# Layer 0 of a two-layer graph network: where the preparation and output stages stand among a step's matrix products

## The chip, the cores and the metric

The kernel runs on one core of a Trainium2 chip (trn2). The metric is device time in microseconds (us) of one execution; of several executions the median is taken. Five engines work side by side on a core and meet at semaphores: TensorE (PE in the profile, with its weight loads as PEld), VectorE (DVE), ScalarE (ACT), GpSimd (POOL) and SyncE (SP, which issues DMAs here).

## The reference, cut to what matters

The change lies wholly in layer 0, which is a graph attention layer over 3327 nodes with 256 features and 4 heads of 64 features, applied to a normalized input:

```python
h = maximum(layernorm(x), 0)
support = (h @ weight) per head                    # n x 64 for each of 4 heads
f1, f2 = support . weight_u, support . weight_v    # one number per node and head
e = exp(leaky_relu(f1[None, :] + f2[:, None], 0.2) - row maximum), where adj != 0, else 0
out = (e / sum of e over the row) @ support + bias + h @ proj_w.T + proj_b
x = x + out
```

Layer 1 (two steps of attention cut to its largest weights, with a second, smoothing path over the graph) takes the rest of the time and isn't touched.

The kernel uses that exp(leaky_relu(z)) is max(exp(z), exp(0.2 z)). A factor that belongs to the row alone cancels in the division, so the weight of neighbour j for node i is exp(0.2 f1[j]) times max(exp(0.8 f1[j]), exp(-0.8 f2[i])). The tiles are named `eas` for exp(0.2 f1), `cf` for exp(0.8 f1) and `ef` for exp(-0.8 f2), which is spread over the partitions into `xf0`.

## The kernel before, in words

Layer 0 works on the transposed matrix: partitions are 128 neighbours j (26 tiles, the last of 127 rows), columns are nodes i. The columns come in four blocks (`BLOCKS`) of 6, 8, 8 and 4 tiles, that is 768, 1024, 1024 and 511 columns. The main loop (L961) runs over `order`: 4 blocks times 26 tiles j, 104 steps. The sums over j are held in PSUM for the whole of a block.

A step does this, in the order in which it is written:

- The adjacency tile for three steps ahead is loaded (`load_adj`, SP queue) and the present one is copied to `adj_r` in DRAM (POOL queue).
- `weigh` (L913, DVE instruction at L920) makes the weights of heads 0 and 1. Each is one DVE instruction over all columns of the block. The weights go round in a ring of seven buffers (`weights`, L661 and L662). In the trace these buffers are called `lg` and `w`. A step uses four of them, so the fourth head of a step (h = 3) takes the buffer that head 0 of the step just before held; heads 0 to 2 take buffers of the step before that one.
- DVE then does what has been put between the heads. In block 0 that is `take(i - 1)` (L740; L742, L748, L749), which moves the features of a later tile from PSUM into `sup` and `res`, and in every second step `stats` (L679; L683 and L684) of two tiles. In blocks 1 to 3 it is what `on_dve` holds for the step (L980): parts of the output of the block before.
- `weigh` makes the weights of heads 2 and 3.
- PE does `sum_features(accs, j, 0)` (L922, product at L928), the weighted sum of features of heads 0 and 1. Two heads stand side by side in 64 columns each of the PE array.
- PE does the preparation and output stages. In block 0 `features(i, 7)` (L710; L714, L716, L718) multiplies a later tile by the layer's weights, i = j + 8. In blocks 1 to 3 it is what `on_pe` holds for the step (L988).
- PE does `sum_features(accs, j, 1)`, the same sum for heads 2 and 3.
- In block 0 PE does `turn(i + 1, 6)` (L698, transposes at L703).
- PE does `sum_weights(accs, j)` (L933, product at L938), the sum of the weights of all four heads, four of them side by side in 32 columns each. It is the last reader of the step's weight buffers.

When a block is finished, its sums are copied out (L1006) and each of its tiles of 128 nodes becomes an `Out`, whose stages are spread over steps of the next block by lines 1008 to 1026: `divide` on PE (L765), a step later `output` on DVE, POOL and ACT (L773 to L788, L790 to L792, L797), then `turn` on PE (L813, copied by ACT at L817), `keys` on PE (L823, ACT L442), `take_keys` on DVE (L444) in the step after, `graph` on PE (L849, ACT L853 and L855) and `take_graph` on DVE (L865) in the step after that. In blocks 1 and 2 this makes a cycle of three steps for each tile: `keys` of one tile with `divide` of the next, then a step with nothing on PE, then `graph` with `turn`. In block 3 eight tiles share 26 steps of half the length, so that steps without any such stage are rare.

The order on PE, DVE, ACT and POOL is the order in which the program is written (`in_traced_order`, L385). An engine whose next instruction has to wait holds up everything behind it. Layer 1's order comes from a planner (`Order`) with costs fixed in the source; it does not depend on the order in layer 0.

Of the kernel before, what the change touches and what calls it, by code (L numbers as in the profile page):

```python
# [312 lines left out]
def kernel(  # L313
# [34 lines left out]
    def rows(i):  # L348
        return min(P, N - i * P)
# [56 lines left out]
    def move_rows(queue, dst, src, pn):  # L406

        for p0, p1 in ((0, pn // 16 * 16), (pn // 16 * 16, pn)):
            if p0 < p1:
                queue.dma_start(out=dst[p0:p1], in_=src[p0:p1])  # L410
# [198 lines left out]
    def bank(k, shape, name="pt"):  # L609
        return banks.tile(shape, FP, tag=f"b{k}", name=name)  # L610
# [14 lines left out]
    if True:  # L625
# [33 lines left out]
        HP = H // 2  # L659
# [19 lines left out]
        def stats(g0):  # L679
            g1 = min(g0 + 2, NT)  # L680
            for i in range(g0, g1):
                st = small.tile([P, 6], FP, tag="ln_st", name="st")
                nc.vector.bn_stats(st, res[:, i, :])  # L683
                nc.vector.bn_aggr(mv[:, i, :], st)  # L684
            g, n = nc.gpsimd, slice(g0, g1)
            g.tensor_scalar(rs[:, n], mv[:, n, 1], EPS, None, ALU.add)
            g.tensor_tensor(rs[:, n], rs[:, n], mhalf.to_broadcast([P, g1 - g0]), ALU.pow)
            g.tensor_tensor(nmr[:, n], mv[:, n, 0], rs[:, n], ALU.mult)
            g.tensor_scalar(nmr[:, n], nmr[:, n], -1.0, None, ALU.mult)
# [3 lines left out]
        def normalize(i):  # L693
            normed[i] = hn = turn_of(spare)
            nc.scalar.activation(
                hn, res[:, i, :], AF.Relu, bias=nmr[:, i : i + 1], scale=rs[:, i : i + 1]
            )
# [12 lines left out]
        def features(i, k):  # L710
            hT, pt = turned.pop(i)
            f1, f2, pw = pt[:, D : D + H], pt[:H, D + H : D + H + P], bank(k, [P, 2, D])
            for c in range(DC):
                nc.tensor.matmul(f1, hT[:, c], wuv[:, c, 0], start=(c == 0), stop=(c == DC - 1))  # L714
            for c in range(DC):
                nc.tensor.matmul(f2, wuv[:, c, 1], hT[:, c], start=(c == 0), stop=(c == DC - 1))  # L716
            for c in range(DC):
                nc.tensor.matmul(pw, hT[:, c], wcat[:, c], start=(c == 0), stop=(c == DC - 1))  # L718
            t0, t1 = next(s for s in SPREADS if s[0] <= i < s[1])
            nc.scalar.activation(eas[:, i], f1, AF.Exp, scale=SLOPE)  # L720
            nc.scalar.activation(cf[:, i], f1, AF.Exp, scale=1.0 - SLOPE)
            nc.scalar.activation(ef[:, i - t0], f2, AF.Exp, scale=SLOPE - 1.0)
            if i == t1 - 1:
                spread(t0, t1, ef)
            made[i] = pw
# [14 lines left out]
        def take(i):  # L740
            pw = made.pop(i)
            nc.vector.tensor_tensor(  # L742
                sup[:, i].rearrange("p (h o) -> p h o", h=H),
                pw[:, 0].rearrange("p (h o) -> p h o", h=H),
                eas[:, i].unsqueeze(2).to_broadcast([P, H, O]), ALU.mult,
            )
            t = pa.tile([P, D], FP, tag="xu", name="t")
            nc.vector.tensor_add(t, pw[:, 1], res[:, i])  # L748
            nc.vector.tensor_add(res[:, i], t, badd)  # L749
# [163 lines left out]
        def weigh(j, at, b, cn, *heads):  # L913
            pj = rows(j)
            for h in heads:
                ws[h] = w = turn_of(weights)
                cw = -(-cn // P) * P
                cb = xf0[b][:pj, :, h * P : (h + 1) * P].bitcast(FP)
                a, o = (t[:pj, :cw].rearrange("p (t n) -> p t n", n=P) for t in (at, w))
                nc.vector.scalar_tensor_tensor(o, cb, cf[:pj, j, h : h + 1], a, ALU.max, ALU.mult)  # L920

        def sum_features(accs, j, p):  # L922
            pj = rows(j)
            for m, acc in enumerate(accs[p]):
                mn = min(512, cn - 512 * m)
                for q in range(2):
                    h = 2 * p + q
                    nc.tensor.matmul(  # L928
                        acc[q * O : (q + 1) * O, :mn], sup[:pj, j, h * O : (h + 1) * O],
                        ws[h][:pj, 512 * m : 512 * m + mn], start=(j == 0), stop=(j == NT - 1),  # L930
                    )
# [14 lines left out]
        def load_adj(b, j):  # L946
            c0, pj = BLOCKS[b][0] * P, rows(j)
            cn = min(BLOCKS[b][1] * P, N) - c0
            ats[b, j] = at = turn_of(rows_of_adj)
            if cn % P:  # L950
                nc.gpsimd.memset(at[:, cn : -(-cn // P) * P], 0.0)
            move_rows(nc.sync, at[:, :cn], adj_t[j * P : j * P + pj, c0 : c0 + cn], pj)
# [8 lines left out]
        for step, (b, j) in enumerate(order):  # L961
            c0 = BLOCKS[b][0] * P
            cn = min(BLOCKS[b][1] * P, N) - c0
            if j == 0:
                ws = {}
                half = range((cn + 511) // 512)
                accs = [[bank(len(half) * p + m, [P, 512]) for m in half] for p in range(HP + 1)]
            at = ats.pop((b, j))
            if step + 3 < len(order):
                load_adj(*order[step + 3])  # L970
            move_rows(
                nc.gpsimd, adj_r[j * P : j * P + rows(j), c0 : c0 + cn], at[:, :cn], rows(j)
            )
            i = j + AHEAD
            weigh(j, at, b, cn, 0, 1)
            if b == 0 and AHEAD < i <= NT:
                take(i - 1)
            if b == 0 and i % 2 == 0 and i + 4 < NT:
                stats(i + 4)
            for f in on_dve.pop(step, ()):  # L980
                f()
            weigh(j, at, b, cn, 2, 3)
            if b == 0 and i + 2 < NT:
                normalize(i + 2)
            sum_features(accs, j, 0)
            if b == 0 and i < NT:
                features(i, 7)
            for f in on_pe.pop(step, ()):  # L988
                f()
            sum_features(accs, j, 1)  # L990
            if b == 0 and i + 1 < NT:
                turn(i + 1, 6)
            sum_weights(accs, j)
            if j < NT - 1:
                continue
            if b == 0:
                ug = p0.tile([P, DC, 2, D], FP, tag="by", name="ug")
                for n in range(STEPS):
                    nc.sync.dma_start(
                        out=ug[:, :, n, :],  # L1000
                        in_=u1t[STEPS - 1 - n].rearrange("(c p) j -> p c j", p=P),
                    )
            for p in range(HP + 1):
                for m, acc in enumerate(accs[p]):
                    mn = min(512, cn - 512 * m)
                    nc.scalar.copy(ot[:, p, 512 * m : 512 * m + mn], acc[:, :mn])  # L1006
            outs = [Out(c0 // P + t, ot, t * P) for t in range((cn + P - 1) // P)]
            if b < NB - 1:
                last = b == NB - 2
                for k, r in enumerate(outs):  # L1010
                    a = step + 1 + (1 + 13 * k // 5 if last else 1 + 3 * k)
                    ka, kb, kc = ((3, 4)[k % 2], (5, 6)[k % 2], 7) if last else (6, 7, 6)
                    g = a + (5 if last or k < WIDE - 1 else 4)
                    for when, f in (
                        (a, lambda r=r, ka=ka: r.divide(ka)),
                        (a + (3 if last else 2), lambda r=r, kb=kb: r.turn(kb)),
                        (a + (4 if last else 3), lambda r=r, kb=kb: r.keys(kb)),
                        (g, lambda r=r, kc=kc: r.graph(kc)),
                    ):
                        on_pe.setdefault(when, []).append(f)  # L1020
                    for when, f in (
                        (a + 1, r.output),
                        (a + (5 if last else 4), lambda r=r: (r.take_keys(), r.store_keys())),
                        (g + 1, lambda r=r: (r.store_sum(), r.take_graph(), r.store_graph())),
                    ):
                        on_dve.setdefault(when, []).append(f)
# [784 lines left out]
```

## Time and profile before

| what | value |
|---|---|
| median of 3 runs | 2047.48 us (2043.74 to 2048.77) |
| the profiled execution's own time | 2044.76 us |
| its span, first to last instruction | 2042.7 us |
| mean granted clock of TensorE | 0.989 |
| busy PE / DVE / ACT / POOL over the span | 1964.5 / 1679.8 / 1305.6 / 782.7 us |
| main loop of layer 0, block 0 (26 steps of 768 columns) | 42.3 to 214.0 us |
| block 1 (26 steps of 1024 columns) | 214.0 to 378.0 us |
| block 2 (26 steps of 1024 columns) | 378.0 to 546.1 us |
| block 3 (26 steps of 511 columns) | 546.1 to 655.5 us |

The block limits are the starts of the first L928 product of each block and the end of the last L938. In the timeline a row is an instruction or several of one kind in a row: its start in us from the start of the span, its duration, the engine, the line, the operation, output and inputs, shapes and count, and in square brackets the idle time of the engine before it with what ended it. Each fp32 product appears as two PE instructions, so eight L928 rows are one `sum_features` of a block of two 512-column halves. PE's instructions overlap by some 0.07 us; where this text gives the length of a stage on PE, it is the time from its first start to the first start of the next stage.

### The profile page before, as it was taken

What the parts mean: (1) busy time and instruction counts of PE and PEld (TensorE: products, weight loads), DVE (VectorE), ACT (ScalarE), POOL (GpSimd) and SP (SyncE); (2) the same over time, 40 slices, a digit from 0 to 9 for tenths busy, and PEclk for the clock granted to TensorE, in tenths of its full rate; (3) what the DMA queues carried; (4) which work ended last, traced back from release to release, by engine and by line L of the source; (5) the groups of instructions that cost most, each with busy time, mean ns of one, the idle gap of its engine ahead of it and who ended that gap; (6) DMA issues with size and microseconds to landing.
All of it is one profiled execution on the core that took longest, in us unless ns stands there. A gap on an engine that the chain in (4) does not pass through costs nothing. (4 is left out here: it accounts for less than half of the span.)

```text
span 2042.7 us, 34326 instructions
## 1 busy us (share of the span) xinstructions
PE 1964.5 (96%) x11474; PEld 1384.4 (68%) x11474; DVE 1679.8 (82%) x3997; ACT 1305.6 (64%) x2014; POOL 782.7 (38%) x1842
## 2 busy tenths in 40 slices
PE   7999999999999799999999999995999999999996
PEld 3343333233223688888888888884889999999995
DVE  5777988988788597888889798944899999999994
ACT  2110100010112889999998999839899999999991
POOL 3230222133233443334443435405545455444442
PEclk9999999999999999999999999997999999999998
DMA  5445566565565643433334343566243444444440
GB/s 182 144 157 168 191 220 229 172 204 190 177 189 155 175 110 99 107 90 78 93 94 113 80 103 79 142 199 199 64 119 99 107 109 106 109 108 103 102 113 23
DMA packets 324157, 270.60 MB, mean 132 GB/s; under 512 B 30260, under 2 KB 300563, under 8 KB 323972
## 3 DMA queue, kind: packets, MB, share of 16 engines
q1 hardware_dynamic: 311284, 222.85, 40.4%
q0 software_dynamic: 11520, 44.81, 6.2%
q8 instruction: 92, 1.51, 0.3%
q14 instruction: 93, 0.76, 0.1%
q10 hardware_dynamic: 1168, 0.67, 0.1%
HBM read 177.79 MB, written 88.62 MB: 130 GB/s over the span
## 5 line engine op out<-in xcount | busy, mean ns | idle before, releaser
L1218 ACT ACTIVATE at<-lg,at 128x3327 fp8e4<-128x3327 f32 x208 | 638.9, 3072 | 5.1 <-POOL at L1178 2.5
L1072 PE MATMUL accr<-xf,adjt 128*128 128x258 f32 (+3 forms) x1352 | 375.6, 309 | 34.3 <-DMA adjt<-adj_r 18.2
L920 DVE SCALAR_TENSOR_TENSOR lg<-xf,cf,at 128x1024 f32<-128x1024 f32 (+4 forms) x357 | 368.3, 1078 | 45.3 <-PE pt L938 44.9
L1073 PE MATMUL accr<-xf,adjt 128*128 128x256 f32 (+1 forms) x1352 | 343.5, 285 | 1.9 <-DMA xf<-xf_d 1.9
L928 PE MATMUL pt<-lg,sup 128*64 128x512 f32 (+3 forms) x1250 | 335.3, 574 | 1.1 <-DVE lg L920 1.0
L1357 PE MATMUL acca<-res,at 128*128 128x256 f32 (+2 forms) x1352 | 321.7, 379 | 0.0
L1357 PE MATMUL acca<-xa,at 128*128 128x256 f32 (+2 forms) x1352 | 321.1, 379 | 0.0
L1072 PEld LDWEIGHTS accr<-xf,adjt 128*128 128x128 f32 (+1 forms) x1352 | 259.5, 192 | 46.4 <-DMA adjt<-adj_r 18.1
L1073 PEld LDWEIGHTS accr<-xf,adjt 128*128 128x128 f32 (+1 forms) x1352 | 260.5, 193 | 9.3 <-DMA xf<-xf_d 2.5
L1357 PEld LDWEIGHTS acca<-res,at 128*128 128x128 f32 (+2 forms) x1352 | 245.3, 190 | 31.2 <-issue 3.4
L1357 PEld LDWEIGHTS acca<-xa,at 128*128 128x128 f32 (+2 forms) x1352 | 245.6, 190 | 28.3
L1152 POOL TENSOR_SCALAR sc<-sc 128x1 f32<-128x1 f32 (+1 forms) x156 | 34.7, 249 | 476.8 <-ACT sc L1150 476.5
L1133 PE MATMUL pg<-k_sb,q 128*128 128x512 f32 (+2 forms) x728 | 209.8, 407 | 3.8 <-ACT lg L1142 3.2
L928 PEld LDWEIGHTS pt<-lg,sup 128*64 128x64 f32 (+1 forms) x1250 | 92.1, 136 | 176.3 <-issue 116.4
L1284 DVE MAX8 v<-lg 128x8 f32<-128x416 f32 (+2 forms) x416 | 209.9, 577 | 0.1
L1346 ACT COPY at<-pt 128x512 f32<-128x512 f32 (+2 forms) x247 | 128.2, 531 | 65.2 <-PE acca L1357 35.8
L938 PE MATMUL pt<-lg,eas 128*32 128x512 f32 (+3 forms) x1250 | 166.4, 568 | 0.0
L1133 PEld LDWEIGHTS pg<-k_sb,q 128*128 128x128 f32 (+1 forms) x728 | 124.7, 189 | 32.6 <-ACT lg L1142 12.2
L1142 ACT COPY lg<-pg 128x512 f32<-128x512 f32 (+2 forms) x249 | 126.7, 571 | 17.3 <-PE pg L1133 14.9
L1275 DVE SCALAR_TENSOR_TENSOR lg<-sup,th 128x3327 f32<-128x3327 f32 (+1 forms) x35 | 128.9, 3682 | 10.1 <-ACT th L1268 9.9
L1336 PE MATMUL pt<-ident,sup 128*128 128x128 f32 (+2 forms) x910 | 129.4, 276 | 4.0 <-DVE sup L1323 3.6
L1323 DVE SCALAR_TENSOR_TENSOR sup<-sup,vm 128x3327 f32<-128x3327 f32 (+1 forms) x35 | 128.9, 3682 | 0.1
(197 smaller groups left out, 3196.0 us busy)
## 6 DMA issues: line engine op xcount, KB each, us to landing
adjt<-adj_r SPq DMA_DIRECT2D x300, 256.0 KB, 3.1
at<-in_adj_t_dram SPq DMA_DIRECT2D x50, 512.0 KB, 4.3
adj_r<-at POOLq DMA_DIRECT2D x50, 512.0 KB, 5.4
at<-in_adj_t_dram SPq DMA_DIRECT2D x25, 384.0 KB, 3.2
adj_r<-at POOLq DMA_DIRECT2D x25, 384.0 KB, 3.2
qk_d<-qk SPq DMA_DIRECT2D x50, 128.0 KB, 2.7
q<-qk_d SPq DMA_DIRECT2D x100, 64.0 KB, 2.4
xf_d<-xf SPq DMA_DIRECT2D x50, 128.0 KB, 4.1
```

Of the source, the lines that this page charges most:

```text
L920: nc.vector.scalar_tensor_tensor(o, cb, cf[:pj, j, h : h + 1], a, ALU.max, ALU.mult)
L928: nc.tensor.matmul(acc[q * O : (q + 1) * O, :mn], sup[:pj, j, h * O : (h + 1) * O], ws[h][:pj, 512 * m : 512 * m + mn], start=(j == 0), st ...
L938: nc.tensor.matmul(acc[h * QP : (h + 1) * QP, :mn], eas[:pj, j, h : h + 1].to_broadcast([pj, QP]), ws[h][:pj, 512 * m : 512 * m + mn], sta ...
L1072: nc.tensor.matmul(r.acc[:pn, :dx], w, xc[:, :dx], start=begin, stop=False)
L1073: nc.tensor.matmul(r.acc[:pn, :D], w, xc[:, DX:], start=False, stop=end)
L1133: nc.tensor.matmul(r.pg[p][:pn, :mn], r.q[:, v, :pn], k_sb[:, m0 : m0 + mn], start=(v == 0), stop=(v == 1),)
L1218: nc.scalar.activation(junk[:pn], r.lg[:pn, :N], AF.Exp, bias=r.at[:pn, 4:], accum_out=r.g[:pn], saturate=False,)
L1275: nc.vector.scalar_tensor_tensor(r.lg[:pn, :N], e, r.th[:pn], e, ALU.is_lt, ALU.mult, accum_out=r.below[:pn])
L1284: nc.vector.max(r.v8[:pn, q], r.lg[:pn, q * w : min((q + 1) * w, N)])
L1323: nc.vector.scalar_tensor_tensor(e, e, r.vm[:pn, 1:], e, ALU.is_ge, ALU.mult, accum_out=kept[:pn])
L1336: nc.tensor.transpose(r.pt[g][: rows(c), j, : r.pn], r.e[: r.pn, c * P : c * P + rows(c)], ident[: r.pn, : r.pn],)
L1357: nc.tensor.matmul(r.acc[: r.pn], wt[: rows(c), j, : r.pn], xa[: rows(c), c, :], start=(c == 0), stop=(c == NT - 1),)
```

## The change

The stages on PE that stood between the two feature sums are put behind both of them, ahead of the sum of weights. The sum of features of heads 2 and 3 follows at once on that of heads 0 and 1; in block 0 `turn(i + 1, 6)` then follows at once on `features(i, 7)`.

```diff
             weigh(j, at, b, cn, 2, 3)
             if b == 0 and i + 2 < NT:
                 normalize(i + 2)
-            sum_features(accs, j, 0)
+            for p in range(HP):
+                sum_features(accs, j, p)
             if b == 0 and i < NT:
                 features(i, 7)
             for f in on_pe.pop(step, ()):
                 f()
-            sum_features(accs, j, 1)
             if b == 0 and i + 1 < NT:
                 turn(i + 1, 6)
             sum_weights(accs, j)
```

The order of instructions on DVE, ACT and POOL is the same in both kernels, and PE has the same products in another order. On SP the store of `p_d` and one of the two stores of `xf_d` change places for three tiles. The moved stages carry with them what they issue on other engines: the exponentials of `features` (L720 to L722) and, in five steps, the five DMAs of `spread` (L727); the copies of `turn`, `keys` and `graph` on ACT.

## The prediction

> **What bounds the kernel now.** I read the busy time by windows first, cut at the limits of the blocks, then the waits between 42.3 and 655.5 us, then the timelines of PE and DVE step by step.
>
> ```profile
> core 0: us, PE busy (x) PEld busy (x) DVE busy (x) ACT busy (x) POOL busy (x), PEclk, DMA share, GB/s
> 42.30:180.70 138.40, 138.40 (x826) 54.85 (x826) 97.99 (x156) 20.50 (x86) 35.89 (x49) 1.00 0.45 142
> 546.10:655.50 109.40, 109.25 (x529) 30.66 (x525) 89.59 (x183) 17.20 (x45) 37.52 (x81) 1.00 0.59 179
> ```
>
> PE is busy in every microsecond of layer 0, DVE in 71% of the first window and 82% of the last. So layer 0 is bound by PE, but DVE is close behind. What DVE waits for, the waits tell:
>
> ```profile
> DVE lg L920 <- PE pt L938: 44.9, 57, 1.6
> DVE sup L742 <- PE pt L718: 27.8, 17, 1.6
> ```
>
> DVE waits for PE to free the seventh weight buffer (the fourth head of a step can start only after the weight sums of the step before), and in block 0 `take` waits for the very product `features` has just made. DVE's idle time isn't free slack: it is tied at both ends to PE. Block 0, a step of PE, and the DVE work made from it, with `stats` in it:
>
> ```profile
> 98.26 0.61 PE L714 MATMUL pt<-wuv,hT 128*128 128x4 f32 x4
> 99.33 1.98 PE L718 MATMUL pt<-wcat,hT 128*128 128x512 f32 x4
> 101.25 1.51 PE L928 MATMUL pt<-lg,sup 128*64 128x512 f32 x8
> 102.69 0.44 PE L703 MATMUL pt<-ident,lg 128*128 128x128 f32 x2
> 103.06 1.50 PE L938 MATMUL pt<-lg,eas 128*32 128x512 f32 x16
> 104.48 1.51 PE L928 MATMUL pt<-lg,sup 128*64 128x512 f32 x8
> ```
>
> ```profile
> 101.42 0.42 DVE L742 TENSOR_TENSOR sup<-pt,eas 128x256 f32<-128x256 f32 x1 [1.63 <-PE pt L718]
> 103.64 0.99 DVE L920 SCALAR_TENSOR_TENSOR w<-xf,cf,at 128x768 f32<-128x768 f32 x1
> ```
>
> A step is 7.66 us with no gap on PE. `take` starts 3.16 us after `features` does (98.26 to 101.42). The weights of heads 2 and 3 of the next step are made behind it, and PE's next SF1 (I call the feature sums SF0 and SF1, the weight sums SW) comes late enough: it has SF1, `turn`, SW, SF0 and another `features` before it.
>
> **What the Trainium skill says.** TensorEngine Tiling (Array Packing), Key Properties: changing the tiling mode drains the array. The trace agrees: SF0 and SF1 of 768 columns last 2.73 us when they follow each other (steps with nothing between) and 1.44 each when a stage in full-array mode stands between, so splitting costs 2 x 1.44 - 2.73 = 0.15; at 1024 columns 2 x 1.87 - 3.58 = 0.16, at 511 columns 2 x 1.01 - 1.90 = 0.12. TensorE: Matmul & The Clock Gate, the section on the array as 16 sub-arrays (queue depths): only weight loads may be pulled ahead on PE, matmuls stay in order, and ACT and DVE are strict FIFO. So a late SF1 holds up all stages behind it; the trace shows every PE stage in the order of the program. Same page, Part 1: the clock falls only after an idle window of about 3.4 us; the longest wait that I derive is 2.3 us, and the clock stood at 1.00 in all of layer 0, so I count no slower clock; no run here shows the threshold.
>
> **Part 1, what is saved.** One mode change and back per step that has stages in the middle: 18 steps of block 0, and by the schedule of lines 1008 to 1026 14, 17 and 24 of blocks 1, 2 and 3. That is 73 x 0.15 = 11.0 us. In block 0 `turn` now follows `features` in the same mode: L718 takes 1.82 instead of 1.91 (as it does from 18 to 37 us, where the two stand together) and `turn` 0.31 instead of 0.37 (as L813 behind L849 does): 17 x 0.15 = 2.5. Together 13.5 us. For the 55 steps of blocks 1 to 3 the change from full array into 32 columns (instead of 64) is new. `turn` before SW shows it: 0.37 (102.69 to 103.06), the same as L813 into 64 columns (397.14 to 397.51), so I count no difference; the bounds are 0.09 less (no change of mode at all, 1.82 against 1.91) and 0.09 more, 5 us in all.
>
> **Part 2, what is lost.** The stage moves 1.3 to 1.9 us later, and SF1 of the next step loses that much distance from it. If DVE has work made from the stage, the next SF1 waits whenever DVE's chain is longer than PE's way from the start of the stage to that SF1. DVE's chain ends with two weights: start spacing 0.93, 1.195 or 0.665 and duration 1.02, 1.28 or 0.745 (768, 1024, 511 columns), and 0.055 to PE (at 429.36 a weight ends and at 429.41 its product starts). PE's way is the rest of the stages, SW (1.43, 1.85, 0.99) and SF0 followed by SF1 (1.29, 1.715, 0.89).
>
> Block 0, from the start of `features`: DVE 3.16 + `take` 1.13 + 0.93 + 1.02 + 0.055 = 6.30, with `stats` (1.09) 7.39. PE: `features` 0.54 + 0.53 + 1.82, `turn` 0.31, SW 1.43, SF0 1.29 = 5.92. The wait is 0.38 in 12 steps and 1.47 in 6; one more, behind the last `features` without `turn`, is 0.60. Sum 14.0, less 18 x 0.15 + 2.5 = 5.2 saved: **+8.7**. That this step's SF1 needs its own head 3 is no further limit: that weight starts 0.09 after SW ends.
>
> Blocks 1 and 2:
>
> ```profile
> 422.90 0.71 PE L823 MATMUL pt<-hT,wqk 128*128 128x128 f32 x4
> 423.87 1.94 PE L928 MATMUL pt<-lg,sup 128*64 128x512 f32 x8
> 424.72 0.34 DVE L444 SCALAR_TENSOR_TENSOR qk<-pt,centres,qk 128x128 fp32r<-128x128 f32 x1
> 424.98 0.15 DVE L773 TENSOR_SCALAR rden<-pt 128x4 f32<-128x4 f32 x1
> 426.90 2.45 DVE L920 SCALAR_TENSOR_TENSOR lg<-xf,cf,at 128x1024 f32<-128x1024 f32 x2
> ```
>
> From the start of `keys` (422.90) its ACT copy starts at +0.75 and takes 0.37, L444 follows 0.03 later and takes 0.26 to the next start, the output 1.92 (424.98 to 426.90), then the weights: 0.75 + 0.40 + 0.26 + 1.92 + 1.195 + 1.28 + 0.055 = 5.86. PE: `keys` 0.55, `divide` 0.42, SW 1.85, SF0 1.715 = 4.54. Wait 1.32, today 0.10 (the sums at 427.59 take 3.68 instead of 3.58). Behind `graph` and `turn`: DVE 2.70 to `take_graph` (415.18 to 417.88), 0.34, 1.195, 1.28, 0.055 = 5.57; PE 1.82 + 0.31 + 1.85 + 1.715 = 5.70: no wait. The first tile of each block has `divide` alone: 0.75 + 1.92 + 1.195 + 1.28 + 0.055 = 5.20 against 0.48 + 1.85 + 1.715 = 4.05, 1.16 instead of today's 0.3. The first `keys` of block 1 has L440 and L441 in its chain as well (today's wait 1.02); it grows by the same 1.2. Block 1 has 5 full cycles, block 2 has 7. Block 1: 5 x 1.20 + 0.85 - 14 x 0.15 = **+4.8**; block 2: 7 x 1.20 + 0.85 - 17 x 0.15 = **+6.7**.
>
> Block 3, where steps are short and DVE's work per tile isn't:
>
> ```profile
> 579.78 1.98 PE L849 MATMUL pt<-ug,hT 128*128 128x512 f32 x4
> 582.02 1.08 PE L928 MATMUL pt<-lg,sup 128*64 128x511 f32 x4
> 582.48 0.42 DVE L865 TENSOR_TENSOR xf<-pt,xf 128x256 fp32r<-128x256 f32 x1 [0.46 <-ACT xu L855]
> 584.67 2.71 DVE L920 SCALAR_TENSOR_TENSOR lg<-xf,cf,at 128x512 f32<-128x512 f32 x4
> ```
>
> After `graph`: 2.70 + `take_graph` 0.34 + output 1.92 + 0.665 + 0.745 + 0.055 = 6.43 against PE 1.82 + `divide` 0.42 + 0.99 + 0.89 = 4.12: wait 2.30 (twice); with a `turn` of 0.22 too 2.08 (three times). `graph` alone: 4.51 against 3.79, 0.71 (four). `divide` alone: 0.75 + 1.92 + 1.47 = 4.14 against 2.36, 1.77 to 1.83 (three). `keys`: 1.15 + 0.26 + 1.47 = 2.88 against 2.52, 0.35 (eight). Sum 21.9; today's waits in these sums are 3.4 (at 554.53 0.99, at 585.45 and 620.06 0.65 each, and so on), and 24 x 0.15 = 3.6 is saved: **+14.9**.
>
> Part 3, edits at nothing. ACT's share of the moved stages lies on an engine busy 20.50 of 138.40 us. `turn` reuses the bank of `features`' first products, whose last reader on ACT (L722) ends at 99.81; `turn` would come at 99.33 + 1.82 = 101.15, so 1.3 us cover it. The DMAs of `spread` and of `take_keys` go out some 2 us later; the first is used only in the next block, the second in layer 1. The three swapped stores on SP are read in layer 1. POOL's three operations before a `relu` start with DVE's output; `turn` comes two steps later and more.
>
> Sum: 8.7 + 4.8 + 6.7 + 14.9 = 35.1. Against the profiled execution 2044.8 + 35 = 2079.8. That one lies 2.7 below the median of the runs (2047.5) and inside their range of 5 us; the median with the sum is 2082.6. I take 2081. Layer 1 begins when PE ends layer 0, so I carry the delay through; its first waits for `adjt` loads (10.6 us of PE in 655.5 to 760) could give back at most a part.
>
> **Rivals.** A, faster: DVE gets done earlier, because its 45 us of waiting absorb the delay, and only the mode changes remain: 2044.8 - 13.5 = 2031. For it speaks the idle DVE; against it that the idle time comes before the fourth head or before `take`, and `take` starts only when `features` ends. It decides where DVE's chain is under PE's way: 0.38 us in block 0, 1.32 in blocks 1 and 2. B, less: the waits in block 3 aren't as regular as derived (one late SF1 gives the next weights time), and half of 14.9 is lost: 2081 - 7.5 = 2073.5. C, more: waits feed each other, a late `relu` makes `turn` and `keys` late as well; say each of the 20 waits of a full cycle or of over 1.7 us grows by 0.5: 2081 + 10 = 2091. I saw `turn` with two microseconds and more to spare.
>
> **How the numbers follow.** Forecast 0.76, A 0.05, B 0.11, C 0.08. The forecast's own range is about 2076 to 2086 (the runs' spread of 5 us and half of the 5 us on either side for the new change into 32 columns). To hold 8 in 10 and most of B, 2072 to 2089. A difference of 0.3% (6 us) is about what a measurement of this kernel can tell: faster 0.05, same 0.02, slower 0.93.
>
> **What would show it.** Right: SF1 (L928) has idle time ended by DVE L920 in nearly every step with a stage, 0.38 and 1.47 in turn in block 0; block 0 ends 9, block 1 14, block 2 20 and block 3 35 us later than now; DVE's waits for L938 shrink. Wrong: steps of block 0 of 7.36 us (then A), or waits at L813 and L823 in layer 0 (then C).

## The result, and the profile after

| | before | changed |
|---|---|---|
| median of 4 runs each | 2048.12 us (2043.74 to 2052.10) | 2083.98 us (2080.60 to 2086.04) |
| profiled execution, its span | 2044.76, 2042.7 us | 2083.28, 2081.1 us |
| ratio | | 1.0174, 95% interval 1.0149 to 1.0199 |

The changed kernel is 36 us slower. The time is in layer 0's main loop, block by block as forecast. Each length is taken from the first L928 of the block to the first L928 of the next (block 3: to the first L765 after it).

| | predicted | measured |
|---|---|---|
| block 0 | +8.7 | +9.7 (42.28 to 213.97; 43.14 to 224.51) |
| block 1 | +4.8 | +4.1 |
| block 2 | +6.7 | +6.5 |
| block 3 | +14.9 | +14.4 |
| main loop | +35.1 | +34.7 |

Of the remaining 3.8 us between the two profiled executions, 0.9 lie before the loop and 2.9 behind it (1387.2 against 1390.1 us), in code that is the same. Other executions with the old order show the same spread: 1390.3 in e8 below.

The windows of the changed kernel that answer to those of before (block 0's steps with `features`, and block 3):

```profile
core 0: us, PE busy (x) PEld busy (x) DVE busy (x) ACT busy (x) POOL busy (x), PEclk, DMA share, GB/s
43.10:190.70 147.60, 145.90 (x828) 62.12 (x828) 96.06 (x156) 20.56 (x86) 35.70 (x49) 0.99 0.43 133
567.30:691.00 123.70, 115.55 (x529) 34.23 (x525) 89.44 (x183) 18.16 (x48) 37.33 (x81) 1.00 0.53 160
```

In block 3 the same 529 products take 123.7 us instead of 109.4, and PE shows 8 us of idle time. In block 0 the 18 steps with `features` take 147.6 us instead of 138.4, and PE shows only 1.7 us of idle time. The reason is that two heads run side by side: when the weight of one is there and that of the other isn't, the first runs alone. PE counts as busy and has half its columns empty. Such a wait is seen in the length of a stage, not in the idle time.

The waits of the changed kernel over the main loop (43.1 to 691 us):

```profile
PEld pt L928 <- DVE lg L920: 81.2, 117, 2.2
DVE xf L865 <- ACT xu L855: 55.1, 22, 2.9
DVE sup L742 <- PE pt L718: 50.4, 18, 3.0
DVE lg L920 <- PE pt L938: 11.5, 28, 0.9
PE pt L928 <- DVE lg L920: 9.7, 14, 1.4
```

Two of these waits in the kernel before (42.3 to 655.5 us); the other two stand in the prediction:

```profile
PEld pt L928 <- DVE lg L920: 41.1, 67, 1.1
DVE xf L865 <- ACT xu L855: 20.8, 22, 2.4
```

DVE's wait for the freed weight buffer falls from 44.9 to 11.5 us. Its waits for what a stage on PE has made rise, from 27.8 to 50.4 for `take` and from 20.8 to 55.1 for `take_graph`. DVE does no more work than before (1677.7 us busy over the span instead of 1679.8); its idle time has moved from a place where it cost nothing to one ahead of the weights that PE needs next. Weight loads for the feature sums now wait 81.2 us for DVE's weights instead of 41.1.

Block 0 of the changed kernel, a step without `stats` and one with them, first PE, then DVE:

```profile
102.78 3.16 PE L928 MATMUL pt<-lg,sup 128*64 128x512 f32 x16
105.87 0.61 PE L714 MATMUL pt<-wuv,hT 128*128 128x4 f32 x4
108.76 0.38 PE L703 MATMUL pt<-ident,lg 128*128 128x128 f32 x2
109.07 1.50 PE L938 MATMUL pt<-lg,eas 128*32 128x512 f32 x16
110.50 1.51 PE L928 MATMUL pt<-lg,sup 128*64 128x512 f32 x8
112.29 1.07 PE L928 MATMUL pt<-w,sup 128*64 128x512 f32 x2 [0.28 <-DVE w L920]
114.65 0.61 PE L714 MATMUL pt<-wuv,hT 128*128 128x4 f32 x4
```

```profile
111.25 0.99 DVE L920 SCALAR_TENSOR_TENSOR w<-xf,cf,at 128x768 f32<-128x768 f32 x1
112.15 2.87 DVE L920 SCALAR_TENSOR_TENSOR lg<-xf,cf,at 128x768 f32<-128x768 f32 x3
117.81 0.42 DVE L742 TENSOR_TENSOR sup<-pt,eas 128x256 f32<-128x256 f32 x1 [2.79 <-PE pt L718]
```

The two sums last 3.09 us (102.78 to 105.87) and 4.15 us (110.50 to 114.65) instead of the 2.73 that they take undisturbed, so SF1 waits 0.36 and 1.42 us; predicted were 0.38 and 1.47. Head 2's weight ends at 112.24, 0.05 ahead of its product at 112.29. Only 0.28 of the wait is idle time of PE: head 2 runs alone until head 3's weight is there (113.16), and the end of head 3 runs alone.

A step of block 2 with `keys` and `divide`, and the step after it, PE and DVE:

```profile
440.52 0.71 PE L823 MATMUL pt<-hT,wqk 128*128 128x128 f32 x4
441.07 0.49 PE L765 MATMUL pt<-ident,ot 128*128 128x128 f32 x3
443.34 4.95 PE L928 MATMUL pt<-lg,sup 128*64 128x512 f32 x16
448.22 1.92 PE L938 MATMUL pt<-lg,eas 128*32 128x512 f32 x16
```

```profile
441.67 0.35 DVE L444 SCALAR_TENSOR_TENSOR qk<-pt,centres,qk 128x128 fp32r<-128x128 f32 x1 [0.82 <-ACT qk L442]
443.86 2.45 DVE L920 SCALAR_TENSOR_TENSOR lg<-xf,cf,at 128x1024 f32<-128x1024 f32 x2
```

L444 starts 1.15 us after `keys`, as soon as ACT's copy is there. In the old order it started 1.82 us after `keys` (422.90 to 424.72), behind a weight that DVE had still to make, and was early enough. Now it is late, and the two weights behind it end at 446.31. The sums last 4.88 us (443.34 to 448.22) instead of 3.58: a wait of 1.30, predicted 1.32. Block 3, behind a step with `graph` and `divide`:

```profile
608.99 0.64 PE L928 MATMUL pt<-lg,sup 128*64 128x511 f32 x1
611.42 1.73 PE L928 MATMUL pt<-lg,sup 128*64 128x511 f32 x4 [1.36 <-DVE lg L920]
613.09 0.44 PE L813 MATMUL pt<-ident,res 128*128 128x128 f32 x2
```

```profile
608.45 0.42 DVE L865 TENSOR_TENSOR xf<-pt,xf 128x256 fp32r<-128x256 f32 x1 [2.43 <-ACT xu L855]
610.65 3.37 DVE L920 SCALAR_TENSOR_TENSOR lg<-xf,cf,at 128x512 f32<-128x512 f32 x5
```

The sums take 4.10 us (608.99 to 613.09) instead of 1.90: 2.20, predicted 2.30.

### The profile page after: what moved, and what is told of

It reads as the page before. It is cut to its first block, busy times and chain, and to the rows that moved or that the text cites. A ratio compares the mean times of both kernels' runs of the same rounds, so it can differ in the third digit from the quotient of the medians.

```text
span 2081.1 us, 34314 instructions
## 1 busy us (share of the span) xinstructions
PE 1993.6 (96%) x11474; PEld 1404.9 (68%) x11474; DVE 1677.7 (81%) x3997; ACT 1305.9 (63%) x2014; POOL 784.2 (38%) x1842
## 5 line engine op out<-in xcount | busy, mean ns | idle before, releaser
L920 DVE SCALAR_TENSOR_TENSOR lg<-xf,cf,at 128x1024 f32<-128x1024 f32 (+4 forms) x357 | 365.8, 1076 | 11.6 <-PE pt L938 11.5
L928 PE MATMUL pt<-lg,sup 128*64 128x512 f32 (+3 forms) x1250 | 348.1, 575 | 10.9 <-DVE lg L920 9.7
L1072 PEld LDWEIGHTS accr<-xf,adjt 128*128 128x128 f32 (+1 forms) x1352 | 263.1, 195 | 46.4 <-DMA adjt<-adj_r 19.1
L1073 PEld LDWEIGHTS accr<-xf,adjt 128*128 128x128 f32 (+1 forms) x1352 | 264.2, 195 | 9.1 <-DMA xf<-xf_d 2.3
L928 PEld LDWEIGHTS pt<-lg,sup 128*64 128x64 f32 (+1 forms) x1250 | 102.3, 136 | 220.9 <-issue 103.2
```

The costliest lines, as they stand in the source:

```text
L928: nc.tensor.matmul(acc[q * O : (q + 1) * O, :mn], sup[:pj, j, h * O : (h + 1) * O], ws[h][:pj, 512 * m : 512 * m + mn], start=(j == 0), st ...
L1072: nc.tensor.matmul(r.acc[:pn, :dx], w, xc[:, :dx], start=begin, stop=False)
L1073: nc.tensor.matmul(r.acc[:pn, :D], w, xc[:, DX:], start=False, stop=end)
```

## The experiments

The theory: an SF1 waits for DVE's weights because the stage from which DVE's work is made has come too near to it. The rivals: the order on PE itself costs (changes of mode), or DVE can't run ahead because the ring has only seven buffers. "Main loop" below is the profiled difference to the kernel before, summed over blocks as in the table above; medians and ratios are against the kernel before on the same chip (2047.2 us for e1 to e4, 2047.8 for e5 to e8, 2048.3 for e9).

**e1 and e2, the change in two parts.** In e1 the second sum goes ahead in block 0 only, in e2 in the other blocks only:

```diff
             sum_features(accs, j, 0)
+            if b == 0:                       # e1
+                sum_features(accs, j, 1)
             if b == 0 and i < NT:
                 features(i, 7)
+            if b > 0:                        # e2
+                sum_features(accs, j, 1)
             for f in on_pe.pop(step, ()):
                 f()
-            sum_features(accs, j, 1)
+            if b > 0:                        # e1; in e2: b == 0
+                sum_features(accs, j, 1)
```

> The stages are moved in block 0 alone (features, and turn behind it); blocks 1 to 3 keep the old order. Theory (the next SF1 loses its distance from the stage that DVE's work is made from, so it waits for the weights of heads 2 and 3): the same waits in block 0 as in the changed kernel, 0.36 and 1.42 us in turn, and none of the new ones later; 9.7 us slower than before (the changed kernel ended block 0 10.5 later, of which 0.9 came before the first step), so about 2058. Rival (the order on PE itself costs, and most of that in the new change of mode from full array into 32 columns): block 0 has that change in the old order as well, so that only the saved mode change would be left there, 2043, and the whole loss would lie in blocks 1 to 3.

> The stages are moved in blocks 1 to 3 alone. Theory: the waits of these blocks are those of the changed kernel (1.3 us in each cycle of blocks 1 and 2, up to 2.3 us in block 3); 25 us slower than before, about 2073, and with the first part it adds up to the whole. Rival (a late block 0 is what disturbs the later blocks): clearly less than 25.

e1: 2055.81 us, ratio 1.0041 (1.0028 to 1.0053); block 0 +9.45, the others within 0.04. e2: 2073.08 us, ratio 1.0124 (1.0104 to 1.0144); blocks 1 to 3 +4.11, +6.51, +14.38, which are the changed kernel's +4.12, +6.50, +14.38 to 0.01. The parts add up, and what a block loses does not depend on what comes before it. That the loss lies only where a new change of mode appears is refuted by e1.

**e3, more buffers.** The changed kernel, with the ring's memory cut anew at the start of each block (`wide` holds the three pieces of memory):

```diff
             if j == 0:
                 ws = {}
+                cw = -(-cn // P) * P
+                weights[:] = [t[:, k : k + cw] for t in wide for k in range(0, t.shape[1] - cw + 1, cw)]
```

> The changed kernel with the same memory for the weights cut by the width of the block, so that block 0 has nine buffers and block 3 fourteen (blocks 1 and 2 keep seven). Rival (the seventh buffer is the limit: DVE can't run ahead, so it is late for SF1): the waits in blocks 0 and 3 go, about 25 us of the loss comes back, about 2059. Theory: DVE's waits for L938 go in these blocks, but take and the output still start only when their stage on PE ends, so SF1 waits as before; within 2 us of the changed kernel, 2084.

Measured: 2085.63 us, ratio 1.0183 (1.0163 to 1.0202), no better than the changed kernel. Block 0 of e3 on DVE (its line numbers are one higher):

```profile
101.63 3.80 DVE L921 SCALAR_TENSOR_TENSOR lg<-xf,cf,at 128x768 f32<-128x768 f32 x4
108.22 0.42 DVE L743 TENSOR_TENSOR sup<-pt,eas 128x256 f32<-128x256 f32 x1 [2.79 <-PE pt L719]
```

Four weights run without a wait for a buffer, and then DVE stands 2.79 us before `take`, as with seven buffers. The sums last 3.09 and 4.15 us again, and block 3 loses 14.2. The ring isn't the limit here. The new cut itself costs 2.8 us at the start of block 1 (1.1 of them just ahead of its first product) and 0.9 us at that of block 2, where a new buffer overlaps two old ones.

**e4, the same order on PE, another on DVE.**

```diff
             weigh(j, at, b, cn, 0, 1)
+            weigh(j, at, b, cn, 2)
             if b == 0 and AHEAD < i <= NT:
                 take(i - 1)
...
-            weigh(j, at, b, cn, 2, 3)
+            weigh(j, at, b, cn, 3)
```

> The order on PE of the changed kernel; on DVE what stands between the weights of heads 1 and 2 (take, stats, the output stages) is put between those of heads 2 and 3, so that one weight instead of two lies behind it. Theory: DVE's chain is shorter by one weight (0.93, 1.2 or 0.67 us): the waits in block 0 go from 0.36 and 1.42 to 0 and 0.5, in blocks 1 and 2 from 1.3 to 0.1, in block 3 they shrink by 0.67; 1.8 us slower than before, about 2050. Rival (order on PE and mode changes): nothing changes on PE, so about 2084.

Measured: 2050.23 us, ratio 1.0011 (1.0003 to 1.0020). By blocks -0.7, -1.2, -1.4 and +5.6, together +2.3. The sums of the first step of block 0, and of a later step that waits for `stats`, with the start of the stage behind them:

```profile
41.97 2.99 PE L928 MATMUL pt<-lg,sup 128*64 128x512 f32 x10 [0.98 <-DVE lg L920]
45.82 1.50 PE L928 MATMUL pt<-lg,sup 128*64 128x512 f32 x6 [0.86 <-DVE lg L920]
47.26 0.61 PE L714 MATMUL pt<-wuv,hT 128*128 128x4 f32 x4
59.24 3.29 PE L928 MATMUL pt<-lg,sup 128*64 128x512 f32 x16
62.46 0.61 PE L714 MATMUL pt<-wuv,hT 128*128 128x4 f32 x4
```

After the first step the sums last 2.73 us, and 3.22 (59.24 to 62.46) where `stats` stands before them: waits of 0 and 0.49. The order on PE is that of the changed kernel; moving one weight on DVE takes away 34 us. So the order on PE isn't what costs. The first step is an exception: its sums last 5.29 us (41.97 to 47.26), because SF1 comes before DVE has made the weight of head 3. This step is 1.34 us longer than in the kernel before.

**e7 and e8, the disputed work doubled.** `stats` in the main loop goes twice over its two tiles (seven times 1.09 us more on DVE), e7 in the changed kernel, e8 in the one before:

```diff
-            for i in range(g0, g1):
+            for i in (*range(g0, g1), *(range(g0, g1) if g0 > AHEAD else ())):
```

> The changed kernel with the seven stats of block 0's main loop done twice on DVE (1.09 us more each; the result is the same). Theory: DVE's chain bounds these steps, so each of the seven costs its full 1.09 us: 7.6 us slower than the changed kernel, about 2091. Rival (PE's order bounds): hidden, 2084.

> The kernel before with the same seven stats done twice. Theory: here SF1 lies far enough from features that 1.09 us more on DVE still fit: no difference, 2048. If it costs 7 us here too, DVE bounds block 0 in both orders, and the distance lost is not what matters.

e7: 2089.72 us, ratio 1.0207 (1.0192 to 1.0223); block 0 is 7.2 us longer than in the changed kernel (7.6 were expected), and the sums that wait for `stats` last 5.20 instead of 4.15:

```profile
114.44 1.51 PE L928 MATMUL pt<-lg,sup 128*64 128x512 f32 x8
117.28 1.07 PE L928 MATMUL pt<-w,sup 128*64 128x512 f32 x2 [1.33 <-DVE w L920]
119.64 0.61 PE L714 MATMUL pt<-wuv,hT 128*128 128x4 f32 x4
```

e8: 2045.45 us, ratio 0.9993 (0.9985 to 1.0002); no step of block 0 but the first, in which the clock fell (last section), differs from before. The same DVE work is hidden in the old order and costs nearly its full price in the new one.

**e5, e6 and e9, built from the theory.** All three have `take` and `stats` behind the weight of head 3. e5 moves PE's stages in blocks 0 to 2 only and has the output stages on DVE between heads 2 and 3. e6 has the changed kernel's order on PE in all blocks, the output stages behind head 3 in block 3, and e3's cut; e9 is e6 with that cut at the start of block 3 alone.

```diff
             weigh(j, at, b, cn, 0, 1)
+            weigh(j, at, b, cn, 2)
+            done = on_dve.pop(step, ())
+            for f in done if b < NB - 1 else ():      # e5: in every block
+                f()
+            weigh(j, at, b, cn, 3)
+            for f in done if b == NB - 1 else ():     # not in e5
+                f()
             if b == 0 and AHEAD < i <= NT:
                 take(i - 1)
             if b == 0 and i % 2 == 0 and i + 4 < NT:
                 stats(i + 4)
-            for f in on_dve.pop(step, ()):
-                f()
-            weigh(j, at, b, cn, 2, 3)
```

> Built from the theory to beat both: stages moved behind both feature sums in blocks 0 to 2, old order in block 3; on DVE take and stats behind head 3, the output stages between heads 2 and 3. With the distances so, following the chains step by step leaves no wait in block 0 (4.1 us faster there), the saved mode changes in blocks 1 and 2 (2.6 us), and 2.1 us in block 3: 8.8 us faster than before, about 2039. If mode changes save nothing, 2045 to 2048.

> Stages moved in all blocks; take and stats behind head 3; output stages between heads 2 and 3 in blocks 1 and 2, behind head 3 in block 3; and the weights' memory cut by the width of the block (nine buffers in block 0, fourteen in block 3), so that DVE may run ahead where its work stands behind head 3. Theory: the same order on PE as the changed kernel that was 36 us slower, here 11.8 us faster than before, about 2036. Rival (order on PE): not under 2070.

> As e6_all_moved_dve_late, but the weights' memory is cut anew at the start of block 3 alone. In e6 the first steps of blocks 1 and 2 lost 2.8 and 0.9 us, where a new buffer overlaps two old ones and has to wait for both. Theory: that loss goes, blocks 0 to 2 gain 6.7 us over before and block 3 4.5 to 5.6; 11 to 12 us faster than before, about 2036. If the loss in e6 had another cause, 2038.5 again.

e5: 2038.46 us, ratio 0.9954 (0.9940 to 0.9967). e6: 2038.54 us, ratio 0.9953 (0.9939 to 0.9966). e9: 2036.74 us, ratio 0.9947 (0.9934 to 0.9961), 11.5 us faster than before; by blocks -4.2, -1.2, -1.2 and -4.5. e6 fell 2.6 us short of its expectation; the starts of its blocks 1 and 2 lose the 2.8 and 0.9 us that e3 shows for the cut. e9, without the cut there, loses nothing at these places and came close to its expectation. No run has e9's order in block 3 without the finer cut, so what the cut adds there isn't shown. A step of block 0 in e9:

```profile
107.48 0.38 PE L704 MATMUL pt<-ident,lg 128*128 128x128 f32 x2
109.22 2.80 PE L929 MATMUL pt<-lg,sup 128*64 128x512 f32 x16
111.95 0.61 PE L715 MATMUL pt<-wuv,hT 128*128 128x4 f32 x4
```

The sums last 2.73 us, the step 7.36 instead of 7.66. So the saving of Part 1, 0.30 us a step, is real; in the changed kernel it lies under the waits.

## Why the prediction was right

2081 was forecast, 2083.98 measured. The sum for the main loop was 35.1, the trace has 34.7. Point by point:

- *Bound by PE, with DVE's idle time tied at both ends.* Right. e8 shows the room in the old order, e7 that there is none in the new. Rival A, which took DVE's 45 us of waiting for slack, fell: that wait shrank by 33 us and paid for nothing, since it came before the work that is late and not between it and its user.
- *Part 1, 13.5 us saved.* Right where it can be seen alone: e9's steps of 7.36 us, and 0.15 us in each step of blocks 1 and 2 with stages in it and no wait. The change from full array into 32 columns costs what into 64 does: `divide` behind `keys` lasts 0.42 (441.07 to 441.49) as it did (423.45 to 423.87). The bound of 5 us wasn't needed.
- *Part 2, the waits.* The two chains gave each wait to 0.1 us in most places: 0.38, 1.47, 1.32, 2.30 predicted, 0.36, 1.42, 1.30, 2.20 measured. They do not show as the prediction's sign said, as idle time at L928 in nearly every step with a stage, but in the length of the sums. Two terms were too large. Behind `divide` alone the output was taken to start 0.75 us after `divide`; it starts 0.59 after it (233.59 to 234.18), so these steps grew by 0.65 instead of 0.85 in blocks 1 and 2, and waited 1.5 instead of 1.8 in block 3. Behind the first `keys` of block 1 a step grew by 0.69 instead of 1.2: in the old order DVE was still making a weight when `keys` was done, and L440 started 1.93 us after `keys`; it now starts 0.76 after, so DVE's way became shorter too.
- *Block 0.* 9.7 was measured instead of 8.7, in part by another way. Steps 1 to 18 lost 8.1 where 8.6 was forecast. The other 1.6 came in the first step, for which the sum has next to nothing (a wait of 0.38 less the saving; only 11 of its 12 such waits lie behind a `features` of the loop). In this step SF1 used to have `features` before it and now follows SF0 at once, while `stats` still stands before the weights of heads 2 and 3: head 3's weight ends at 46.94, its product starts at 47.00. e4 lost 1.34 in this step by such a wait, at full clock. In the changed kernel the clock fell as well (last section), which leaves about 0.2 us for it.
- *The sum.* That 35.1 and 34.7 agree so closely is partly luck: without the first step the loop lost 33.1 where 35.0 was forecast, and the first step gave back 1.5 of the difference. In block 3 the saving was put at 0.15 a step although 0.12 had been read for 511 columns; with 0.12 that block would have come to 15.6, not 14.9. The steps without a wait in the changed kernel are 0.12 to 0.15 shorter.
- *Edits at nothing.* Right as far as seen: no wait at L813 or L823 in the changed kernel beyond their weight loads' issue, so Rival C's late `relu` does not occur; e2's equality with the changed kernel to 0.01 us in blocks 1 to 3 shows that the waits don't feed on each other from block to block. Rival B's half of block 3 isn't there: 14.4 of 14.9.

The medians differ by 35.9 us. That 3 us more than 2081 were measured is within the spread of the code that is the same in both (1387.2 to 1391.1 us behind the loop over all the executions here).

## What to carry to other kernels

Before moving work on the busiest engine, follow two ways from the start of the moved stage to the next instruction that waits: through the other engine (what it makes from the stage, and all that is queued behind that in its order), and through the busy engine itself. The difference is the wait, and idle time elsewhere on the other engine does not count against it. If the order is better on the one engine, move its partner's work on the other with it: the same order on PE was 36 us slower with DVE's order kept and 11.5 us faster with it adapted (and the ring cut finer in block 3).

## What the runs showed of the hardware

The clock. In the profiles of the changed kernel, e1, e2, e3 and e5 to e8 the granted clock stood at half for 3.4 us near the start of the main loop (from 44.1 us in the changed kernel), in those of before, e4 and e9 it did not. The first sums of e2, then of the kernel before, both in the old order:

```profile
42.70 3.75 PE L928 MATMUL pt<-lg,sup 128*64 128x512 f32 x8 [0.98 <-DVE lg L920]
42.28 2.43 PE L928 MATMUL pt<-lg,sup 128*64 128x512 f32 x8 [0.98 <-DVE lg L920]
```

In e2 the clock fell at 43.4, and two products of 512 columns then start 0.85 us apart instead of 0.43. PE had not been idle for 3.4 us there: it was busy 1.97 of the 3.4 us up to the fall, with gaps of 0.46 and 0.98. The Trainium skill (TensorE: Matmul & The Clock Gate, Part 1) gives an idle window of about 3.4 us for the fall to half clock, and the prediction took this for the only way; these runs show it fall after a merely thin stretch. The kernel before has the same two gaps at this place and no fall; what decides isn't shown. With the old order the fall cost 1.5 us (e2) and 1.6 us (e8). With the changed kernel's order in block 0 most of it is hidden under the wait for head 3: the first step is 1.34 us longer in e1, with the fall, and in e4, without it. The later waits, up to 2.2 us between dense work, did not bring the clock down in any block.

Half a PE. Products of two heads in 64 columns each run side by side only if both operands are there. If not, one runs alone and PE still counts as busy, so the 18 waits of steps 1 to 18 in block 0, 0.36 to 1.42 us each and 13.1 us together, show as 1.7 us of idle time.
